# Projected keys and queries of an attention kernel: whole 512-column blocks, four block writes per half, separate staging, queries projected at the end of the attention before

## The chip, the cores and the metric

The kernel runs on one core of a Trainium2 chip. A core has five engines that run their own instruction streams in order: TensorE (PE, matrix products into PSUM), VectorE (DVE), ScalarE (ACT), GpSimd (POOL) and SyncE (SP, which here only starts DMA transfers). ScalarE starts DMA transfers on a queue of its own too. The metric is the device time of one execution in microseconds (us), median of three runs.

## The reference

The input x is 4 images of 256 channels by 64 × 64 = 4096 positions, in float32. Two layers follow each other. The second one is told in words only, since the change doesn't touch what it computes.

```python
xf = x.reshape(B, C, N)                                  # 4, 256, 4096
q = jnp.einsum('oc,bcn->bno', wq, xf) + bq               # 32 channels
k = jnp.einsum('oc,bcn->bon', wk, xf) + bk[None, :, None]  # 32 channels
attn = jax.nn.softmax(jnp.einsum('bnd,bdm->bnm', q, k), axis=-1)
v = jnp.einsum('oc,bcn->bon', wv, xf) + bv[None, :, None]  # 256 channels
out = jnp.einsum('bcn,bmn->bcm', v, attn).reshape(B, C, H, W)
y = gamma[0] * out + x
```

The second layer: a group norm, a context cluster block (features and values of 4 heads × 24 channels, split in four folds of 32 × 32 positions, similarity of each position to four centres, a hard assignment to the best one, aggregation, projection back to 256 channels, added with a factor), a second group norm, an MLP 256 → 1024 → 256 with GELU, added with a factor, and at the end batch norms, ReLU and a 256 × 256 pointwise product.

## The kernel before, in words

**Order.** The order of all engines' work is written out by hand (`tc.manual_schedule`): each engine takes its instructions in the order in which the Python code issues them, and waits on semaphores where data or a buffer is not ready. The images run one after the other. Each has an attention stage, a cluster stage (with group norm 1), and an MLP stage (with group norm 2), and work of the next image is put into the gaps of the last two.

**Attention.** An image has 8 query blocks of 512 positions (`nb`) and 8 key groups of 512 positions (`g`). A unit `u` is one pair of these, 64 in all. For each unit `score` (L386 on) multiplies four 128-key slices with the query block on TensorE (sc, L395), and ScalarE copies the result from PSUM to a slot of the pool `spool` (tag "s"), while VectorE keeps a running maximum. `exps` (L500, L503) subtracts the maximum on VectorE and takes the exponential on ScalarE, POOL adds up the denominators (L505, L508), and `weigh` (L513) multiplies by the values on TensorE into PSUM (av). Scores run 10 units ahead of the weighting (`LEAD`). `weighting` is the loop over all 64 units; it loads x of the next image at its end (`ahead`) and the weights of the following stages (`load_mix`, `load_mlp`).

**Split operands.** Keys and queries have 32 channels. Both are held as a rounded part (hi) and the rest (lo), and stacked on 128 partitions: four row groups c of 32 rows, in which keys are hi, lo, hi, lo and queries hi, hi, lo, lo. One product over 128 rows then gives the sum of all four products of the parts.

**Projection and stacking.** `k_half(i)` projects the keys of half an image (2048 positions): 32 rows in each of four row groups r of a PSUM tile (from the pool `ps_m`, 2 banks), each row group holding other positions. `halves_of` forms hi on ScalarE (L298) and lo on VectorE (L299). Since each row group holds other positions, the stacking goes through DRAM: 16 transfers of 64 KB (row group c of the stack by row group r of the projection, L326) on SP's queue write the DRAM tile [128, 4096], and `k_unit` (L381) and `q_block` (L375) load blocks [128, 512] from it. `q_four(i)` does the same for four query blocks (L356, L367). hi and lo of a key half, and those of queries of the first half, share one SBUF tile with the tag "acc" and one buffer, which is the tag of the denominators too. So the next half's hi waits until the 16 writes before it have landed.

**Where these stand.** For image 0, `alone()` runs `k_half(0)`, `q_four(0)`, the first loads, four v pairs (L337 on TensorE, copied by ScalarE at L345), and then eight score units, each followed by a v pair; `k_half(1)` stands before unit 3. For later images, the list `projections` has 32 v half steps, in which `k_half(0)` and `q_four(0)` stand after the 16th and `k_half(1)` after the 26th counted with these; `fill(n)` takes the next n of the list at fixed places of the stages of the image before (tail of the attention, group norms, cluster, first part of the MLP). In every image, `q_four(1)` stands after unit 17 of its own attention.

Of the kernel before, what the change touches and what calls it, by code (L numbers as in the profile page):

```python
# [8 lines left out]
F32 = mybir.dt.float32  # L9
F32R = mybir.dt.float32r  # L10
# [36 lines left out]
def attention_then_cluster_block(  # L47
# [229 lines left out]
    def attention(b, xs):  # L277
# [4 lines left out]
        cells = small.tile([P, KC, NBLK, 4], F32, tag="cells", name=f"cells_{b}")  # L282
        qs, ks, slots, mxs, accs, tops, rdens, ts = {}, {}, {}, {}, {}, {}, {}, {}

        def halves_of(ps, bias, tags, name):

            if len(tags) == 1:  # L290
                both = work.tile([P, 2, NB], F32R, tag=tags[0], bufs=1, name=f"hl_{name}")
                hi, lo = both[:, 0], both[:, 1]
            else:
                hi, lo = (
                    work.tile([P, NB], F32R, tag=t, bufs=1, name=f"hl{j}_{name}")
                    for j, t in enumerate(tags)
                )
            nc.scalar.activation(hi, ps, AF.Identity, bias=bias)  # L298
            nc.vector.scalar_tensor_tensor(  # L299
                lo, ps, bias, hi.bitcast(F32), ALU.add, ALU.subtract  # L300
            )
            return hi, lo

        def k_half(i):

            if i == 0:
                own["k"] = dram.tile([P, N], F32, tag="k", name=f"k_{b}")
                own["q"] = dram.tile([P, N], F32, tag="q", name=f"q_{b}")
            ps = ps_m.tile([P, NB], F32, tag="m", name=f"kp_{b}_{i}")
            for t in range(2):  # L310
                for k in range(KC):
                    for r in range(RG):
                        nc.tensor.matmul(
                            ps[r * D : (r + 1) * D, t * 2 * P : (t + 1) * 2 * P],
                            wqk_s[:, k, 1],
                            xs[2 * i + t][:, k].rearrange("p (g r n) -> p r g n", g=2, r=RG)[:, r],
                            start=(k == 0),
                            stop=(k == KC - 1),
                        )
            parts = halves_of(ps, bqk_s[:, 1:2], ("acc",), f"k_{b}_{i}")  # L320
            cols = own["k"][:, i * N // 2 : (i + 1) * N // 2]
            for c in range(4):
                rows = cols[c * D : (c + 1) * D].rearrange("d (g r n) -> d r g n", r=RG, n=P)
                src = parts[c % 2].bitcast(F32).rearrange("p (g n) -> p g n", n=P)
                for r in range(RG):
                    nc.sync.dma_start(out=rows[:, r], in_=src[r * D : (r + 1) * D])  # L326

        vps = {}

# [18 lines left out]
            v_half(2 * i)  # L348
            v_half(2 * i + 1)

        def q_four(i, tags=("acc",)):

            ps = ps_m.tile([P, NB], F32, tag="m", name=f"qp_{b}_{i}")
            for k in range(KC):
                for r in range(RG):
                    nc.tensor.matmul(  # L356
                        ps[r * D : (r + 1) * D],
                        wqk_s[:, k, 0],
                        block(xs, k, 4 * i + r),
                        start=(k == 0),  # L360
                        stop=(k == KC - 1),
                    )
            parts = halves_of(ps, bqk_s[:, 0:1], tags, f"q_{b}_{i}")
            for c in range(4):
                for r in range(RG):
                    o = (4 * i + r) * NB
                    nc.sync.dma_start(  # L367
                        out=own["q"][c * D : (c + 1) * D, o : o + NB],
                        in_=parts[c // 2][r * D : (r + 1) * D].bitcast(F32),
                    )  # L370

        def q_block(nb):

            qs[nb] = work.tile([P, NB], F32R, tag="q", name=f"q_{b}_{nb}")
            nc.sync.dma_start(out=qs[nb].bitcast(F32), in_=own["q"][:, nb * NB : (nb + 1) * NB])  # L375

        def k_unit(u):

            g = u % GRP
            ks[u] = big.tile([P, NB], F32R, tag="k", bufs=2, name=f"k_{b}_{u}")  # L380
            nc.sync.dma_start(out=ks[u].bitcast(F32), in_=own["k"][:, g * NB : (g + 1) * NB])  # L381

        def score(u, hooks=None, later=None):

# [181 lines left out]

        def alone():

            k_half(0)
            q_four(0)  # L570
            k_unit(0)
            q_block(0)
            q_block(1)
            for i in range(4):
                v_pair(i)
            for u in range(GRP):
                if u == RG - 1:
                    k_half(1)
                hooks, maxima = [], []
                score(u, hooks, maxima)  # L580
                for f in hooks + maxima:
                    f()
                v_pair(u + 4)
            fold(0)
            for i in range(GRP + 4, GRP + 6):
                v_pair(i)
            half["dg"] = across(0)
            v_pair(GRP + 6)
            spread(0, half["dg"])
            v_pair(GRP + 7)  # L590
            exps(0)
            score(GRP)
# [23 lines left out]
                if p % GRP == GRP - 1:  # L616
                    fold(p // GRP)

        def weighting(ahead, fill, early):
            mb, av = None, None  # L620

            biased = {u: (i // KC, i % KC) for i, u in enumerate((3, 4, 5, 6, 20, 28, 36, 44))}
            for u in range(units):
                nb, g = divmod(u, GRP)
                more = nb + 1 < NBLK
                if g == 0:
                    av = [
                        ps_a.tile([P, NB], F32, tag=f"a{c}", name=f"av{c}_{b}_{nb}")
                        for c in range(KC)
                    ]  # L630
                if g + 1 < GRP:
                    exps(u + 1)
                else:
                    gather(nb)
                p = u + LEAD
                if u == units - 4:
                    load_mix(b)
                    load_mlp(b)
                elif u == units - 1:
                    turn_mlp()  # L640
                due(u, 0)
                if p - units > 1:
                    ahead()
                if g == GRP - 1 and more:
                    exps(u + 1)
                weigh(u, av, 0)
                due(u, 1)
                weigh(u, av, 1)
                if nb:
                    if g == 0:  # L650
                        total(nb - 1)
                    elif g == 3:
                        add(nb - 1)
                    elif g == 5:
                        seen(nb - 1)
                    elif g == 7:
                        pooled(nb - 1)
                due(u, 2)
                weigh(u, av, 2)
                if g == GRP - 2 and more:  # L660
                    known(nb + 1, mb)
                due(u, 3)
                if g == GRP - 3 and more:
                    mb = highest(nb + 1)
                weigh(u, av, 3)
                if u == 1:
                    early()
                if u in biased:

                    t, c = biased[u]  # L670
                    nc.scalar.activation(
                        xs[t][:, c], xs[t][:, c], AF.Identity, bias=gbv[:, c : c + 1]
                    )
                if u == 2 * GRP + 1:
                    q_four(1, ("w2", "q4"))
                if g == 3 and nb + 2 < NBLK:
                    q_block(nb + 2)
                if g == GRP - 1 and more:
                    clear(nb, av)
# [41 lines left out]
        parts.score, parts.fold, parts.q_block, parts.k_unit = score, fold, q_block, k_unit  # L721
        parts.maximum, parts.first, parts.exps = maximum, first, exps
        parts.projections = [lambda i=i: v_half(i) for i in range(N // P)]
        parts.projections[26:26] = [lambda: k_half(1)]
        parts.projections[16:16] = [lambda: k_half(0), lambda: q_four(0)]
        return parts


# [872 lines left out]
    with tc.manual_schedule():  # L1601
# [3 lines left out]
        for b in range(B):  # L1605
            xs1, begun = [], []
            nxt = attention(b + 1, xs1) if b + 1 < B else None

            def ahead():
                if nxt and len(xs1) < N // XT:  # L1610
                    xs1.append(load_x(b + 1, len(xs1)))
                elif late and not begun:
                    begun.append(begin())

            begin, todo, gelu = late or (None, list(nxt.projections) if nxt else [], lambda i: None)
            fill = filler(todo)
            stats, cells, rest = here.weighting(ahead, fill, (lambda: None) if b else derived)
            turned = turn_w2(b, not nxt)
            maxima = []
            stats2 = cluster(b, here.xs, stats, cells, rest, fill, gelu, nxt, maxima)  # L1620

            late = mlp(b, here.xs, stats2, fill, nxt, NBLK - (b == B - 2), turned, maxima)
            here = nxt
# [76 lines left out]
```

## Time and profile before

| | |
|---|---|
| time, median of 3 runs | 3352.77 us (3351.12 to 3354.02) |
| time of the profiled execution | 3354.39 us |
| span of the profiled execution | 3352.4 us |
| mean granted TensorE clock | 0.985 |
| TensorE busy | 3236.9 us, 97% of the span |
| VectorE, POOL, ScalarE busy | 2231.0, 1930.9, 1678.8 us |
| key writes `k<-hl_k` | 128 of 64 KB, 1.8 us from issue to landing |
| query writes `q<-hl_q` | 128 of 64 KB, 1.7 us |
| key loads `k<-k` | 256 of 256 KB, 3.0 us |
| query loads `q<-q` | 32 of 256 KB, 3.2 us |

The profile is one execution, recorded by the hardware profiler. Busy time counts the instructions of an engine; the chain of work that ended last is followed back from the last instruction to what released each step. A wait line names the waiting instruction, the one that released it, and then the sum in us, the number of waits and the longest. A timeline line has the start in us from the span's beginning, the duration of the group, the engine and line, the operation, output and inputs, shape and number of instructions; in square brackets stands the idle time before it and what ended it. SPq stands for SP's DMA queue. Names such as kp, qp (projections in PSUM), hl_k, hl_q (their parts), sc (scores), vp (projected values), av (weighted values) are the kernel's tiles without numbers.

### The profile page before, as it was taken

To read this page: it belongs to the slowest core of one execution; us is meant where nothing else is said; L and a number is where in the kernel's file an instruction comes from. 1 tells how busy PE (TensorE), PEld (TensorE's weight loads), DVE (VectorE), ACT (ScalarE), POOL (GpSimd) and SP (SyncE) were. 2 spreads that over 40 slices of the span, in tenths; PEclk is the share of its full clock that TensorE was granted. 3 is DMA by queue.
4 is the path that set the end of the run, shared out by engine and by line. 5 is a ranking of instruction groups with operands and counts; after the bars stand their busy time and mean duration, and the time that the engine had idled before them with its cause. 6 is when DMAs were issued, how large, how long until landed. Compare 5 with 4: busy or idle time off the path is not lost.

```text
span 3352.4 us, 33609 instructions
## 1 busy us (share of the span) xinstructions
PE 3236.9 (97%) x11242; PEld 1943.3 (58%) x11242; DVE 2231.0 (67%) x3570; ACT 1678.8 (50%) x2253; POOL 1930.9 (58%) x1358
## 2 busy tenths in 40 slices
PE   5999999899999999989999999998999999999999
PEld 4444444688644444468864444456884444446786
DVE  2767775567676677466767677746776767765675
ACT  3655553445565555344556455534455555544444
POOL 0566667266466667636636567663664666673664
PEclk8999999999999999999999999999999999999999
DMA  4121112110111111210011111122011121110000
GB/s 141 38 66 38 48 51 87 32 26 29 44 54 54 47 44 41 87 44 24 29 44 51 52 43 54 41 77 48 20 38 54 43 61 38 47 52 1 13 20 26
DMA packets 103133, 154.83 MB, mean 46 GB/s; under 512 B 16336, under 2 KB 41520, under 8 KB 102960
## 3 DMA queue, kind: packets, MB, share of 16 engines
q1 hardware_dynamic: 101936, 151.56, 14.5%
q8 instruction: 89, 1.46, 0.2%
q10 hardware_dynamic: 1024, 1.12, 0.1%
q14 instruction: 84, 0.69, 0.1%
HBM read 118.96 MB, written 33.67 MB: 46 GB/s over the span
## 4 chain that ended last, share of the span: by engine, by line
PE 89%; DVE 4%; SPq 2%; ACT 1%; DMA 1%; issue 1%; POOL 1%; ACTq 0%; DVEq 0%; POOLq 0%
PE av L513 50%; PE mo L1331 9%; PE sc L395 7%; PE hq L1414 5%; PE hp L1414 3%; PE hr L1414 3%; PE fv L910 3%; PE vp L337 2%; PE mo L1315 1%; SPq L326 1%; SPq L367 1%; PE hq_pw L1414 1%; PE pw L1270 1%; PE hr_pw L1414 1%; PE hp_pw L1414 1%
## 5 line engine op out<-in xcount | busy, mean ns | idle before, releaser
L513 PE MATMUL av<-s,v 128*128 128x512 f32 x4096 | 1800.1, 593 | 0.7 <-ACT s L503 0.7
L508 POOL TENSOR_TENSOR acc<-acc,s 128x1024 f32<-128x1024 f32 x448 | 1060.3, 2367 | 500.7 <-ACT s L503 480.3
L513 PEld LDWEIGHTS av<-s,v 128*128 128x128 f32 x4096 | 778.3, 190 | 898.4 <-issue 868.8
L503 ACT ACTIVATE s<-s 128x1024 f32<-128x1024 f32 x512 | 541.0, 1058 | 600.6 <-DVE s L500 580.4
L500 DVE TENSOR_TENSOR s<-s,mb 128x1024 f32<-128x1024 f32 x512 | 595.7, 1205 | 17.4 <-ACT mb L484 15.8
L421 DVE TENSOR_TENSOR top<-sc,top 128x1024 f32<-128x1024 f32 x196 | 239.1, 1220 | 304.0 <-PE sc L395 304.0
L1369 ACT ACTIVATE hs<-hs,pv_s 128x256 f32<-128x256 f32 x496 | 232.5, 503 | 342.8 <-DVE hs L1405 342.8
L395 PE MATMUL sc<-q,k 128*128 128x512 f32 x1024 | 370.9, 484 | 30.9 <-DMA k<-k 24.6
L1331 PE MATMUL mo<-hs,w 128*128 128x256 f32 x1512 | 385.1, 381 | 0.0
L1331 PEld LDWEIGHTS mo<-hs,w 128*128 128x128 f32 x1512 | 283.9, 190 | 46.1 <-ACT hs L1369 6.6
L424 DVE TENSOR_TENSOR top<-sc,top 128x1024 f32<-128x1024 f32 x196 | 240.1, 1225 | 82.2 <-ACT s L417 69.5
L395 PEld LDWEIGHTS sc<-q,k 128*128 128x128 f32 x1024 | 191.1, 191 | 174.4 <-issue 127.4
L417 ACT COPY s<-sc 128x1024 f32<-128x1024 f32 x224 | 224.7, 1003 | 128.5 <-PE sc L395 109.2
L422 ACT COPY s<-sc 128x1024 f32<-128x1024 f32 x224 | 227.6, 1016 | 110.5 <-DVE top L421 74.4
L1405 DVE TENSOR_TENSOR hs<-hq,hs 128x256 f32<-128x256 f32 x496 | 198.3, 421 | 79.2 <-PE hq L1414 68.8
L505 POOL TENSOR_TENSOR acc<-s 128x1024 f32<-128x1024 f32 x32 | 75.9, 2372 | 291.8 <-ACT s L503 291.8
L1338 POOL TENSOR_TENSOR hs<-hs 128x256 f32<-128x256 f32 x108 | 82.4, 763 | 183.0 <-ACT hs L1422 86.0
L337 PE MATMUL vp<-wv_s,x 128*128 128x256 f32 x512 | 137.7, 417 | 39.9 <-ACT v L345 39.3
L337 PEld LDWEIGHTS vp<-wv_s,x 128*128 128x128 f32 x512 | 102.3, 207 | 67.5 <-ACT v L345 43.2
L1414 PE MATMUL hr<-xn,w 128*128 128x256 f32 x496 | 128.4, 381 | 0.5 <-DVE hs L1405 0.5
L1405 DVE TENSOR_TENSOR hs<-hp,hs 128x256 f32<-128x256 f32 x124 | 52.1, 420 | 115.1 <-ACT hs L1422 115.1
L1047 POOL TENSOR_TENSOR x<-cl,x 128x512 f32<-128x512 f32 x32 | 40.0, 1278 | 120.6 <-ACT cl L1046 120.6
(263 smaller groups left out, 3566.3 us busy)
## 6 DMA issues: line engine op xcount, KB each, us to landing
k<-k SPq DMA_DIRECT2D x256, 256.0 KB, 3.0
out<-xn SPq DMA_DIRECT2D x62, 256.0 KB, 2.2
x<-in_x SPq DMA_DIRECT2D x30, 512.0 KB, 6.2
k<-hl_k SPq DMA_DIRECT2D x128, 64.0 KB, 1.8
q<-hl_q SPq DMA_DIRECT2D x128, 64.0 KB, 1.7
q<-q SPq DMA_DIRECT2D x32, 256.0 KB, 3.2
w<-in_w SPq DMA_DIRECT2D x8, 1024.0 KB, 10.1
mr<-row_mx SPq DMA_DIRECT2D x28, 256.0 KB, 3.5
```

Source lines behind the costliest of these rows:

```text
L337: nc.tensor.matmul(vps[0][:, i % 2, :], xs[i * P // XT][:, k, o : o + P], wv_s[:, k, :], start=(k == 0), stop=(k == KC - 1),)
L395: nc.tensor.matmul(halves[r // 2][:, r % 2, :], k_s[:, r * P : (r + 1) * P], q_s, start=True, stop=True,)
L421: nc.vector.tensor_tensor(top, halves[1], top, ALU.max)
L424: nc.vector.tensor_tensor(top, halves[0], top, ALU.max)
L500: nc.vector.tensor_tensor(sh, sh, mxs[nb].unsqueeze(1).to_broadcast([P, 2, NB]), ALU.subtract)
L503: nc.scalar.activation(sh, sh, AF.Exp)
L508: nc.gpsimd.tensor_tensor(acc, acc, s[:, 2 * h : 2 * h + 2], ALU.add)
L513: nc.tensor.matmul(av[c], own["v"][:, RG * g + quarter, c * P : (c + 1) * P], slots[u][:, quarter, :], start=(g == 0 and quarter == 0), st ...
L1331: return nc.tensor.matmul(bank[:, half * HB : (half + 1) * HB], a[:, j], t, start=start, stop=stop)
L1369: nc.scalar.activation(src, src, AF.Gelu_apprx_tanh, bias=pvc("b1", P, j + 4 * (i > 1)))
L1405: nc.vector.tensor_tensor(dst, ps, term, ALU.add)
L1414: nc.tensor.matmul(out, w, x, start=True, stop=True)
```

## The change

The projection, the split and the writes of a half are now one function, `halves_of`, used for keys and queries alike. The keys too are projected by matmuls of 512 columns, one position block in each row group. The DRAM tile is [8, 4, 32, 512], so that each block [128, 512] is contiguous, and a half is written by four transfers of 256 KB, one per row group c of the stack, each over all 128 partitions of hi or of lo. `staged` projects two halves into the two banks of one score PSUM tile (pool `ps_s`) and keeps their hi and lo apart in the four quarters of one slot of `spool`. `keys(i)` keeps hi and lo of a key half in the two "k" buffers.

In image 0, `staged("first")` has the first halves of keys and queries, written on ScalarE's queue, `staged("second")` has the second halves, at unit 0, written on SP's queue, and six v pairs instead of four stand ahead of the units. For later images, the key halves stay in the list of fill steps at the same indices, while all eight query blocks are projected by `staged("queries")` after unit 61 of the attention of the image before (`prepare`). The list has one step less, and `q_four(1)` after unit 17 is gone.

```diff
@@ -282,48 +282,49 @@
         cells = small.tile([P, KC, NBLK, 4], F32, tag="cells", name=f"cells_{b}")
         qs, ks, slots, mxs, accs, tops, rdens, ts = {}, {}, {}, {}, {}, {}, {}, {}
-        def halves_of(ps, bias, tags, name):
-            if len(tags) == 1:
-                both = work.tile([P, 2, NB], F32R, tag=tags[0], bufs=1, name=f"hl_{name}")
-                hi, lo = both[:, 0], both[:, 1]
-            else:
-                hi, lo = (
-                    work.tile([P, NB], F32R, tag=t, bufs=1, name=f"hl{j}_{name}")
-                    for j, t in enumerate(tags)
-                )
+        def halves_of(which, i, parts, ps, dma=nc.sync):
+            col = 1 if which == "k" else 0
+            if which not in own:
+                own[which] = dram.tile([NBLK, 4, D, NB], F32, tag=which, name=f"{which}_{b}")
+            for k in range(KC):
+                for r in range(RG):
+                    nc.tensor.matmul(
+                        ps[r * D : (r + 1) * D],
+                        wqk_s[:, k, col],
+                        block(xs, k, 4 * i + r),
+                        start=(k == 0),
+                        stop=(k == KC - 1),
+                    )
+            bias = bqk_s[:, col : col + 1]
+            hi, lo = parts
             nc.scalar.activation(hi, ps, AF.Identity, bias=bias)
             nc.vector.scalar_tensor_tensor(
                 lo, ps, bias, hi.bitcast(F32), ALU.add, ALU.subtract
             )
-            return hi, lo
-        def k_half(i):
-            if i == 0:
-                own["k"] = dram.tile([P, N], F32, tag="k", name=f"k_{b}")
-                own["q"] = dram.tile([P, N], F32, tag="q", name=f"q_{b}")
+            rows = own[which][4 * i : 4 * i + 4]
+            for c in range(4):
+                part = hi if c in ((0, 2) if which == "k" else (0, 1)) else lo
+                dma.dma_start(out=rows[:, c], in_=part.bitcast(F32))
+        def staged(name, which, dma=nc.sync):
+            st = spool.tile([P, 4, NB], F32R, tag="s", name=f"st_{b}_{name}")
+            ps = ps_s.tile([P, 2, NB], F32, tag="s", name=f"pr_{b}_{name}")
+            for j, (w, i) in enumerate(which):
+                halves_of(w, i, (st[:, 2 * j], st[:, 2 * j + 1]), ps[:, j], dma)
+        def keys(i):
             ps = ps_m.tile([P, NB], F32, tag="m", name=f"kp_{b}_{i}")
-            for t in range(2):
-                for k in range(KC):
-                    for r in range(RG):
-                        nc.tensor.matmul(
-                            ps[r * D : (r + 1) * D, t * 2 * P : (t + 1) * 2 * P],
-                            wqk_s[:, k, 1],
-                            xs[2 * i + t][:, k].rearrange("p (g r n) -> p r g n", g=2, r=RG)[:, r],
-                            start=(k == 0),
-                            stop=(k == KC - 1),
-                        )
-            parts = halves_of(ps, bqk_s[:, 1:2], ("acc",), f"k_{b}_{i}")
-            cols = own["k"][:, i * N // 2 : (i + 1) * N // 2]
-            for c in range(4):
-                rows = cols[c * D : (c + 1) * D].rearrange("d (g r n) -> d r g n", r=RG, n=P)
-                src = parts[c % 2].bitcast(F32).rearrange("p (g n) -> p g n", n=P)
-                for r in range(RG):
-                    nc.sync.dma_start(out=rows[:, r], in_=src[r * D : (r + 1) * D])
+            parts = [
+                big.tile([P, NB], F32R, tag="k", bufs=2, name=f"hl{j}_{b}_{i}") for j in range(2)
+            ]
+            halves_of("k", i, parts, ps)
         vps = {}
@@ -348,37 +349,16 @@
             v_half(2 * i)
             v_half(2 * i + 1)
-        def q_four(i, tags=("acc",)):
-            ps = ps_m.tile([P, NB], F32, tag="m", name=f"qp_{b}_{i}")
-            for k in range(KC):
-                for r in range(RG):
-                    nc.tensor.matmul(
-                        ps[r * D : (r + 1) * D],
-                        wqk_s[:, k, 0],
-                        block(xs, k, 4 * i + r),
-                        start=(k == 0),
-                        stop=(k == KC - 1),
-                    )
-            parts = halves_of(ps, bqk_s[:, 0:1], tags, f"q_{b}_{i}")
-            for c in range(4):
-                for r in range(RG):
-                    o = (4 * i + r) * NB
-                    nc.sync.dma_start(
-                        out=own["q"][c * D : (c + 1) * D, o : o + NB],
-                        in_=parts[c // 2][r * D : (r + 1) * D].bitcast(F32),
-                    )
         def q_block(nb):
             qs[nb] = work.tile([P, NB], F32R, tag="q", name=f"q_{b}_{nb}")
-            nc.sync.dma_start(out=qs[nb].bitcast(F32), in_=own["q"][:, nb * NB : (nb + 1) * NB])
+            nc.sync.dma_start(out=qs[nb].bitcast(F32), in_=own["q"][nb].rearrange("c d n -> (c d) n"))
         def k_unit(u):
             g = u % GRP
             ks[u] = big.tile([P, NB], F32R, tag="k", bufs=2, name=f"k_{b}_{u}")
-            nc.sync.dma_start(out=ks[u].bitcast(F32), in_=own["k"][:, g * NB : (g + 1) * NB])
+            nc.sync.dma_start(out=ks[u].bitcast(F32), in_=own["k"][g].rearrange("c d n -> (c d) n"))
         def score(u, hooks=None, later=None):
@@ -566,24 +546,21 @@
         def alone():
-            k_half(0)
-            q_four(0)
+            staged("first", (("k", 0), ("q", 0)), nc.scalar)
             k_unit(0)
             q_block(0)
             q_block(1)
-            for i in range(4):
+            for i in range(6):
                 v_pair(i)
             for u in range(GRP):
-                if u == RG - 1:
-                    k_half(1)
+                if u == 0:
+                    staged("second", (("k", 1), ("q", 1)))
                 hooks, maxima = [], []
                 score(u, hooks, maxima)
                 for f in hooks + maxima:
                     f()
-                v_pair(u + 4)
+                v_pair(u + 6)
             fold(0)
-            for i in range(GRP + 4, GRP + 6):
-                v_pair(i)
             half["dg"] = across(0)
             v_pair(GRP + 6)
             spread(0, half["dg"])
@@ -616,7 +593,7 @@
                 if p % GRP == GRP - 1:
                     fold(p // GRP)
-        def weighting(ahead, fill, early):
+        def weighting(ahead, fill, early, prepare):
             mb, av = None, None
             biased = {u: (i // KC, i % KC) for i, u in enumerate((3, 4, 5, 6, 20, 28, 36, 44))}
@@ -671,8 +648,8 @@
                     nc.scalar.activation(
                         xs[t][:, c], xs[t][:, c], AF.Identity, bias=gbv[:, c : c + 1]
                     )
-                if u == 2 * GRP + 1:
-                    q_four(1, ("w2", "q4"))
+                if u == units - 3:
+                    prepare()
                 if g == 3 and nb + 2 < NBLK:
                     q_block(nb + 2)
                 if g == GRP - 1 and more:
@@ -721,8 +698,9 @@
         parts.score, parts.fold, parts.q_block, parts.k_unit = score, fold, q_block, k_unit
         parts.maximum, parts.first, parts.exps = maximum, first, exps
         parts.projections = [lambda i=i: v_half(i) for i in range(N // P)]
-        parts.projections[26:26] = [lambda: k_half(1)]
-        parts.projections[16:16] = [lambda: k_half(0), lambda: q_four(0)]
+        parts.projections[26:26] = [lambda: keys(1)]
+        parts.projections[16:16] = [lambda: keys(0)]
+        parts.prepare = lambda: staged("queries", (("q", 0), ("q", 1)))
         return parts
@@ -1614,7 +1592,9 @@
             begin, todo, gelu = late or (None, list(nxt.projections) if nxt else [], lambda i: None)
             fill = filler(todo)
-            stats, cells, rest = here.weighting(ahead, fill, (lambda: None) if b else derived)
+            stats, cells, rest = here.weighting(
+                ahead, fill, (lambda: None) if b else derived, nxt.prepare if nxt else lambda: None
+            )
             turned = turn_w2(b, not nxt)
             maxima = []
             stats2 = cluster(b, here.xs, stats, cells, rest, fill, gelu, nxt, maxima)
```

## The prediction

> **What bounds the kernel now.** I read the page's chain first, then TensorE's waits, then the timeline of each place where the change touches TensorE's order. The chain:
>
> ```profile
> PE 89%; DVE 4%; SPq 2%; ACT 1%; DMA 1%; issue 1%; POOL 1%; ACTq 0%; DVEq 0%; POOLq 0%
> ```
>
> TensorE is busy 3236.9 of 3352.4 us, so an edit pays only as far as it shortens TensorE's own work or its roughly 115 us of gaps. The waits (total us, times, longest) name the gaps of these helpers:
>
> ```profile
> PE vp L337 <- ACT v L345: 39.3, 8, 12.7
> PE sc L395 <- DMA k<-k: 24.6, 5, 10.4
> ...
> PE sc L395 <- DMA q<-q: 4.3, 1, 4.3
> ```
>
> By window, the 39.3 is 12.9 at the start and 9.0, 8.1 and 9.2 in the three passages from one image to the next. ScalarE, named as releaser, is itself held: over all engines `ACT hl_q L298 <- DMA k<-hl_k` is 44.3 us in 4 waits. The timeline of the first passage shows it:
>
> ```profile
> 631.01 1.93 PE L313 MATMUL kp<-x,wqk_s 128*32 128x256 f32 x32
> 632.77 1.90 PE L356 MATMUL qp<-x,wqk_s 128*32 128x512 f32 x16
> 635.25 8.66 SPq L326 DMA_DIRECT2D k<-hl_k  x16
> 645.45 0.69 ACT L298 ACTIVATE hl_q<-qp,bqk_s 128x512 fp32r<-128x512 f32 x1 [10.22 <-DMA k<-hl_k]
> 646.66 3.78 PE L337 MATMUL vp<-wv_s,x 128*128 128x256 f32 x8 [8.61 <-ACT v L345]
> 652.37 3.02 PE L940 MATMUL agg<-vf,sim 128*32 128x96 f32 x64 [1.93 <-DVE sim L870]
> ```
>
> The query half needs the "acc" tile that the key half's 16 writes still read. ScalarE stands 10.2 us; the v copy behind it frees no PSUM bank; TensorE stops. In the middle of an attention (columns as above):
>
> ```profile
> 234.86 1.92 PE L356 MATMUL qp<-x,wqk_s 128*32 128x512 f32 x16
> 237.65 7.37 SPq L367 DMA_DIRECT2D q<-hl_q  x16
> 248.26 1.17 PE L395 MATMUL sc<-q,k 128*128 128x512 f32 x4 [3.49 <-DMA k<-k]
> ```
>
> Here 16 issues hold SP's queue 7.4 us and the next key load is late. And the start:
>
> ```profile
> 19.44 7.72 SPq L326 DMA_DIRECT2D k<-hl_k  x16
> 28.69 0.69 ACT L298 ACTIVATE hl_q<-qp,bqk_s 128x512 fp32r<-128x512 f32 x1 [14.32 <-DMA k<-hl_k]
> 29.41 7.37 SPq L367 DMA_DIRECT2D q<-hl_q  x16
> 42.14 2.04 PE L395 MATMUL sc<-q,k 128*128 128x512 f32 x4 [4.34 <-DMA q<-q]
> 54.40 7.92 SPq L326 DMA_DIRECT2D k<-hl_k  x16
> 66.85 2.05 PE L395 MATMUL sc<-q,k 128*128 128x512 f32 x4 [10.37 <-DMA k<-k]
> 90.80 3.70 PE L513 MATMUL av<-s,v 128*128 128x512 f32 x8 [0.70 <-ACT s L503]
> ```
>
> Up to the first av at 90.8 everything is a serial chain of writes, loads and eight score units.
>
> [...] granted clock 0.50 from 645 to 655 us, and x8 vp matmuls take 3.78 instead of 1.99 us, agg 3.02 instead of 1.50.
>
> **The price of the new write** is the main unknown. 256 KB over four engines is 32 packets of 2 KB each. Near rows: from 813.5 to 816.5, among 2 KB rows, 215 GB/s at DMA share 0.67, so 20 GB/s per engine, 100 ns per packet; the old query writes, two packets per engine at a time, showed 14.6 GB/s (140 ns)[...]; 4 KB rows at 549 to 560 gave 25 GB/s. I take 20: 3.3 us per write, 13 us per half, 26 for two halves. Ends: 2.6 us (25 GB/s) and 4.5 us (14.6 GB/s).
>
> **Part 1: the query half at u = 17 goes** (four attentions). Its matmuls are 1.9 us; the stall behind is 3.49 here and 3.8, 3.4 and 3.5 in the others. 5.4 × 4 = −21.5.
>
> **Part 2: the passage** (three). `keys(0)` has its own two "k" buffers and no query half follows, so the v copy isn't held. The chain from kp to agg(sim), 631.0 to 652.4 = 21.4 us, falls to TensorE's issue of kp, vp, agg(pool_w) and then VectorE's sim chain (5.5 us), which I put at 10.6 in all, with 2.9 us of TensorE idle left: −10.8. [...] the slow clock mostly goes: −1. The fill list is one item shorter, which takes half a v pair out of the MLP's batch: −0.9. About −12.7.
>
> Hidden in it: the 13 us of key writes from about 635 end at 650; `k_0` lands near 657.5 and score(0) needs it at about 662 to 666. Cover some 8 us, gone at about 5 us per write. `keys(1)` waits for the same buffers at about 657: covered by 7 us. The first load behind its writes is for score(1), some 60 us of MLP later.
>
> **Part 3: `prepare()` at u = 61** (three). Two projections at 1.75 us, in TensorE's continuous av run (busy to 590.2), plus a stall where the second half waits for VectorE's lo of the first (both share one PSUM tile: 0.69 + 0.75 and latencies): 1.7. +5.2. ScalarE and VectorE carry two more operations each ahead of the last exponentials, which then end near 586.8 for TensorE's need at 588.5; POOL's last sum ends near 591.6 for the den matmul at 595.3: hidden by 1.7 and 3.7 us. SP issues eight writes; nothing else is in its queue from 563 to 635, and they land by about 606, before the slot's next owner (near 625). Parts 2 and 3: −7.5 × 3 = −22.
>
> **Part 4: the start.** Keys' hi is ready at 14.4; their writes leave on ACT's queue, not behind mix_first, which gains 5 us; but eight writes on four engines take 26.2 us, and ACT's later issues wait for landings of SP's early loads, for which I add 4 to 5: queries land at about 46, `q_0` 3.2 later, score(0) at 49.3 (before: 42.1). `staged("second")` stands ahead of it on TensorE and SP, so its eight writes run from 47 to 75, and `k_1` is behind them: score(1) at 76 (before: 46.1). No key gap follows at unit 4. From score(1): six units at 2.65 us, the pace of 46.09 to 48.75, and 13.4 from score(7) to the first av, as 77.37 to 90.80: 76 + 29.3 is about 105.5, +15. With 2.6 us per write +4, with 4.5 +35 at most: 16 writes in series, 16.5 us per us of the price.
>
> **Sum:** −21.5 − 22 + 15 = −28.5. The profiled execution took 3354.4 with a span of 3352.4; the median is 3352.8. So 3352.8 − 28.5 = 3324.
>
> **Rivals.**
> *All 16 engines carry the writes.* Then a half takes about 4 us, score(1) is at 46.5 as before, the gap at unit 4 goes and first av is at about 74: −17. Total −60: 3292. For it: nothing in this trace shows a transfer on four engines. [...]
> *Loads aren't held by earlier writes.* `k_1` passes them; start −3, total −46: 3306.
> *The passage gives less*: slow writes at 4.5 us, or the gap refilled by VectorE's chain and `prepare()` at double price (+5 × 3): 3335 to 3346.
> *Slower than before: the price of a write at four engines is 5 us or more.* From there the start alone costs 43.5 and eats all the rest (13.1 GB/s per engine, just under the old writes' 14.6). At 6 us: +45 on my sum, 3369. The packets would have to run slower in long rows than in short ones.
>
> **How the numbers follow.** Main case (2.6 to 4 us per write) 0.46, 3313 to 3336; sixteen engines 0.13; loads pass 0.09; passage less 0.20; slow writes 0.12. The likeliest is 3324. The range 3290 to 3350 leaves out the slow writes and the tail of sixteen engines. 0.2% is 6.7 us, about what a measurement of this kernel can tell from no change; below 3346 lie all but the slow writes and a strip of 0.05: faster 0.83, same 0.05, slower 0.12.
>
> **What would show it.** Right: one write on four engines in 3 to 4 us, DMA share near 0.25 from 15 to 75 us, score(1) at 70 to 85 and first av at 100 to 112; no query projection near u = 17 and no key wait of 3.5 there; kp to agg(sim) near 10.6 us; a wait of about 1.7 us at the second query projection. Wrong: DMA share near 1 at the start and first av near 74 (sixteen engines); first av beyond 120; a new wait of den or av at an attention's end; `k_0` late at score(0) of the next image.

## The result and the profile after

| | before | after |
|---|---|---|
| median of 4 runs | 3352.61 us (3351.12 to 3354.02) | 3314.82 us (3314.09 to 3316.30) |
| ratio | | 0.9888, 95% interval 0.9871 to 0.9905 |
| span of the profiled execution | 3352.4 us | 3314.5 us |
| first av product | 90.80 us | 99.85 us |
| mean granted TensorE clock | 0.985 | 0.991 |

The changed kernel is 37.8 us faster. The forecast was 3324, so it had the direction and most of the size; its sum was 9 us short.

The names of the products that serve as marks below: kp is the first product of a key half, den the one that ends an attention, agg(sim) the first product of the cluster stage that needs VectorE's similarities, gnm_gn the first of the second group norm, and hp the first of the MLP. A passage is the stretch from den to hp, with the next image's projections in it.

The chain is TensorE's as before, without the two SPq terms of 1% each. From the page's chain of the changed kernel:

```profile
PE 90%; DVE 5%; DMA 1%; ACT 1%; issue 1%; POOL 1%; SPq 0%; ACTq 0%; DVEq 0%; POOLq 0%
```

TensorE's waits in the changed kernel (us in total, times, longest):

```profile
PE sc L375 <- DMA k<-k: 19.4, 3, 18.3
PE vp L338 <- ACT v L346: 14.2, 4, 12.2
...
PE pr_queries L295 <- DVE st_queries L305: 5.0, 3, 1.7
```

The 39.3 us of vp behind ScalarE's copies are 14.2, nearly all at the start. Of the key waits one, 18.3 us, holds nearly everything, also at the start. The last line is new: the second query projection after unit 61.

**The passage.** Timeline of the changed kernel, first passage (start, us, engine, line, operation):

```profile
639.53 1.92 PE L295 MATMUL kp<-x,wqk_s 128*32 128x512 f32 x16
649.98 1.97 PE L918 MATMUL agg<-vf,sim 128*32 128x96 f32 x64 [2.35 <-DVE sim L848]
```

From kp to agg(sim) are 10.45 us, where 21.36 were. The idle time left is VectorE's, 2.35 us, and agg runs in 1.97 instead of 3.02.

**The attention's end.** Timeline of the changed kernel:

```profile
579.42 1.92 PE L295 MATMUL pr_queries<-x,wqk_s 128*32 128x512 f32 x16
582.18 13.18 SPq L311 DMA_DIRECT2D q<-st_queries  x8
583.00 1.92 PE L295 MATMUL pr_queries<-x,wqk_s 128*32 128x512 f32 x16 [1.65 <-DVE st_queries L305]
598.78 0.43 PE L663 MATMUL den<-rden,ones 128*32 128x128 f32 x8
```

The wait of 1.65 us is there; no wait of av or den follows.

**The start.** Timeline of the changed kernel:

```profile
14.31 3.83 ACTq L311 DMA_DIRECT2D k<-st_first  x4
27.50 4.72 ACTq L311 DMA_DIRECT2D q<-st_first  x4
44.70 3.24 SPq L311 DMA_DIRECT2D k<-st_second  x4
47.37 0.73 PE L375 MATMUL sc<-q,k 128*128 128x512 f32 x2
48.22 10.06 SPq L311 DMA_DIRECT2D q<-st_second  x4
58.33 46.76 SPq L361 DMA_DIRECT2D k<-k  x11
69.78 2.04 PE L375 MATMUL sc<-q,k 128*128 128x512 f32 x4 [18.28 <-DMA k<-k]
99.85 3.70 PE L493 MATMUL av<-s,v 128*128 128x512 f32 x8 [0.71 <-ACT s L483]
```

Score(1) begins at 69.78 instead of 46.09. SP's four query writes alone take 10.06 us to issue, and key 1 is behind them. The windows of the changed kernel (window, its length, busy time and count of PE, PEld, DVE, ACT and POOL, then granted clock, DMA share, GB/s) show how wide the query writes of the first half run:

```profile
35.00:40.00 5.00, 5.00 (x20) 4.19 (x20) 0.00 (x0) 1.17 (x2) 0.53 (x1) 0.80 0.26 102
```

102 GB/s at a share of 0.26 of 16 engines, about what four of them show if they are busy throughout (16 times 0.26 is 4.2). By this estimate each moves 25 GB/s, and 64 KB per engine take 2.6 us.

**Where the 37.9 us of span went**, between anchors of TensorE (first av, each den product, each first MLP product hp), in the order of the stages:

| term | change, us | forecast |
|---|---|---|
| start to first av | +9.05 | +15 |
| attentions, without the projections after unit 61 | −5.7, −8.3, −7.2, −7.6 = −28.8 | −21.5 |
| three times after unit 61: 2 × 1.75 + 1.65 | +15.5 | +15.6 |
| three passages, den to hp: 90.96, 88.24, 90.72 to 78.04, 79.95, 79.97 | −32.0 | −35.4 |
| MLPs with the next scores, hp to av | −0.6 | −2.7 |
| after the last den | −1.0 | 0 |

The attention terms are av-to-den spans (499.47, 501.43, 499.79 and 499.76 before; 498.93, 498.25, 497.77 and 492.16 after), from which the 5.15 us after unit 61 are taken where they occur. The 5.15 is the sum of two products and one wait, read from the timeline.

### The profile page after: what moved, and what is told of

It is laid out like the page before. It is cut to its first block, busy times and chain, and to the rows that moved or that the text cites. A ratio compares the mean times of both kernels' runs of the same rounds, so it can differ in the third digit from the quotient of the medians.

```text
span 3314.5 us, 33083 instructions
## 1 busy us (share of the span) xinstructions
PE 3220.7 (97%) x11114; PEld 1930.3 (58%) x11114; DVE 2231.4 (67%) x3570; ACT 1679.6 (51%) x2253; POOL 1929.9 (58%) x1358
## 4 chain that ended last, share of the span: by engine, by line
PE 90%; DVE 5%; DMA 1%; ACT 1%; issue 1%; POOL 1%; SPq 0%; ACTq 0%; DVEq 0%; POOLq 0%
PE av L493 52%; PE mo L1309 9%; PE sc L375 7%; PE hq L1392 5%; PE hp L1392 3%; PE hr L1392 3%; PE fv L888 3%; PE vp L338 2%; PE mo L1293 1%; PE hq_pw L1392 1%; DVE st L993 1%; PE pw L1248 1%; PE hr_pw L1392 1%; PE hp_pw L1392 1%; DMA k<-k 1%
## 5 line engine op out<-in xcount | busy, mean ns | idle before, releaser
L338 PE MATMUL vp<-wv_s,x 128*128 128x256 f32 x512 | 133.1, 407 | 14.2 <-ACT v L346 14.2
L1392 PEld LDWEIGHTS hr<-xn,w 128*128 128x128 f32 x496 | 94.4, 191 | 18.0 <-issue 3.3
```

The costliest lines, as they stand in the source:

```text
L338: nc.tensor.matmul(vps[0][:, i % 2, :], xs[i * P // XT][:, k, o : o + P], wv_s[:, k, :], start=(k == 0), stop=(k == KC - 1),)
L1392: nc.tensor.matmul(out, w, x, start=True, stop=True)
```

## The experiments

**One: width of the writes.** A layout in which the writes have 128 rows outermost, where the changed kernel's have four blocks, and the loads 32 rows; the number of transfers, their bytes and their places stay.

```diff
-own[which] = dram.tile([NBLK, 4, D, NB], ...)
+own[which] = dram.tile([2, 4, P, NB], ...)
-rows = own[which][4 * i : 4 * i + 4]
+rows = own[which][i]
-dma.dma_start(out=rows[:, c], in_=part.bitcast(F32))
+dma.dma_start(out=rows[c], in_=part.bitcast(F32))
+def stacked(which, nb):
+    r = nb % RG
+    return own[which][nb // RG][:, r * D : (r + 1) * D].rearrange("c d n -> d c n")
-in_=own["q"][nb].rearrange("c d n -> (c d) n")
+in_=stacked("q", nb)
-in_=own["k"][g].rearrange("c d n -> (c d) n")
+in_=stacked("k", g)
```

Keys and queries are then stacked row by row (d, c) instead of (c, d), which changes nothing in their product.

> The changed kernel with one other DRAM layout: [2, 4, 128, 512], so that each of the four writes of a half goes from 128 partitions to 128 rows of one stride [...], and the loads read 32 rows of four row groups each (32 outermost). Count of transfers, their bytes and all places stay. Theory (four engines carry the new writes, and the start pays for it): the writes take about 1 us of their engines instead of 2.6, key 1 is not held, the 18.3 us wait at the start goes, first av near 72 to 76 instead of 99.9, total 3287 to 3293. Rival (the start's loss comes from the place and the order of the writes, not from their width): first av stays near 95 to 100, total within 5 us of 3315.

Measured: 3290.10 us, ratio to before 0.9813 (0.9798 to 0.9827). Timeline of this kernel's start:

```profile
36.38 1.78 SPq L311 DMA_DIRECT2D q<-st_second  x4
...
38.21 36.82 SPq L366 DMA_DIRECT2D k<-k  x11
41.81 1.17 PE L380 MATMUL sc<-q,k 128*128 128x512 f32 x4 [2.16 <-DMA k<-k]
...
69.60 3.70 PE L498 MATMUL av<-s,v 128*128 128x512 f32 x8 [0.71 <-ACT s L488]
```

The windows show the width best after unit 61, where no other transfer is in SP's queue. First the changed kernel, then this one:

```profile
586.00:596.00 10.00, 10.00 (x24) 4.38 (x24) 3.85 (x4) 3.60 (x4) 7.03 (x4) 1.00 0.26 102
554.00:556.00 2.00, 2.00 (x17) 0.56 (x10) 0.00 (x0) 0.24 (x1) 0.00 (x0) 1.00 1.02 379
```

The share of 0.26 has become 1.02, and 102 GB/s have become 379. In the traces' semaphore records the changed kernel's eight writes land there 2.56 us apart and this kernel's 0.7. At the start four issues take 1.78 us instead of 10.06, the 18.3 us wait is 2.16, and the first av comes 30 us earlier than in the changed kernel. The three passages' kp to agg(sim) stay at 10.45. So the start pays for the width, and the width is worth 25 us of the whole. (Of the start's 30 us some 4 come back in this trace, spread over the four attentions, and under 2 in a second trace of the same kernel; why was not tried.)

**Two: number of transfers.** The changed kernel with 16 transfers of 64 KB per half.

```diff
-dma.dma_start(out=rows[:, c], in_=part.bitcast(F32))
+for r in range(RG):
+    dma.dma_start(out=rows[r, c], in_=part[r * D : (r + 1) * D].bitcast(F32))
```

> The changed kernel with 16 transfers of 64 KB per half (32 partitions to 32 rows, as before the change), in the same places and queues. Theory (the count of transfers is worth nothing in itself away from the start, since their issue is hidden): passages and attention as in the changed kernel, kp to agg(sim) near 10.5 us. At the start 32 issues on ScalarE's queue at 0.55 us and 32 on SP's at 0.45 us take the place of the slow writes: first av 92 to 100, total 3307 to 3316. Rival (fewer transfers are what the change lives on): 3325 or more.

Measured: 3310.66 us, ratio 0.9875 (0.9860 to 0.9889). The first av is at 94.35, kp to agg(sim) at 10.45, 10.45 and 10.44. After unit 61, SP issues for 14.89 us and no one waits for it. The timeline of its start shows what the issues cost there:

```profile
13.90 11.38 ACTq L312 DMA_DIRECT2D k<-st_first  x16
...
46.12 7.44 SPq L312 DMA_DIRECT2D k<-st_second  x16
...
53.66 7.43 SPq L312 DMA_DIRECT2D q<-st_second  x16
61.13 38.45 SPq L362 DMA_DIRECT2D k<-k  x11
64.11 2.04 PE L376 MATMUL sc<-q,k 128*128 128x512 f32 x4 [11.19 <-DMA k<-k]
```

With sixteen narrow writes to a half score(1) begins at 64.11 us, with the changed kernel's four at 69.78. Where the changed kernel has them, fewer transfers showed no gain outside the start (kp to agg(sim) 10.45 us with both); at the start 16 issues hold the queue about as long as four slow writes do (7.43 us for each half, against 3.24 and 10.06). At the old place after unit 17 the 16 issues did cost; that is experiment four.

**Three: the passage's wait alone**, in the kernel before. The query half's hi and lo get the two key buffers, for the passages only.

```diff
-parts.projections[16:16] = [lambda: k_half(0), lambda: q_four(0)]
+parts.projections[16:16] = [lambda: k_half(0), lambda: q_four(0, ("k", "k"))]
 ...
+    big.tile([P, NB], F32R, tag=t, bufs=2, name=f"hl{j}_{name}")
+    if t == "k" else
     work.tile([P, NB], F32R, tag=t, bufs=1, name=f"hl{j}_{name}")
```

> The kernel before with one edit: in the passages the query half keeps hi and lo in the two key buffers instead of the tile that the key half's writes still read. The 16 writes per half, the query half at unit 17 and the start stay. Theory (the passage's gap is ScalarE's wait for the key writes to land): kp to agg(sim) falls from 21.4 to about 12, three times about 9 us and 1 to 2 of slow clock, total 3320 to 3328. Rival (the gain of the passage comes from fewer transfers or from the query half's leaving): at most 8 us faster, 3344 or more.

Measured: 3323.91 us, ratio 0.9913 (0.9898 to 0.9928). Timeline of its first passage:

```profile
630.32 1.93 PE L315 MATMUL kp<-x,wqk_s 128*32 128x256 f32 x32
...
634.43 0.67 ACT L300 ACTIVATE hl_q<-qp,bqk_s 128x512 fp32r<-128x512 f32 x1
634.55 8.61 SPq L328 DMA_DIRECT2D k<-hl_k  x16
...
641.42 3.02 PE L942 MATMUL agg<-vf,sim 128*32 128x96 f32 x64 [2.33 <-DVE sim L872]
```

ScalarE takes the query half at once, beside the same 16 writes, and kp to agg(sim) is 11.1 us in all three. The three passages, den to hp, are 29.5 us shorter than before (240.4 instead of 269.9), where the changed kernel has 32.0. The wait for the shared tile was the passage's gap.

**Four: unit 17's stall alone**, in the kernel before: the projection stays and the 16 writes are issued four at a time.

```diff
-q_four(1, ("w2", "q4"))
+held = []
+q_four(1, ("w2", "q4"), held)      # issues the first 4, leaves 3 groups of 4 in held
+elif 2 * GRP + 1 < u < 2 * GRP + 5:
+    held.pop(0)()
-if g == 3 and nb + 2 < NBLK:
+if g == (4 if nb == 2 else 3) and nb + 2 < NBLK:
```

> The kernel before with one edit: of the 16 writes of the query half at unit 17, four are issued after each of units 17, 18, 19 and 20, so that SP is held under 2 us at a time and the key load is not late; the query load of block 4 goes one unit later. The projection itself stays (1.75 us each). Theory from the trace (the stall of 3.5 us also puts TensorE's clock to half for some us in three of four attentions): the stall's 14.2 us go and some 7 more, total 3329 to 3334. Rival (the stall costs only its length): 3337 to 3340.

Measured: 3330.53 us, ratio 0.9933 (0.9916 to 0.9950). No key wait is left in the attentions. The av-to-den spans fall by 3.1, 6.3, 4.9 and 5.3, in sum 19.6 us; the stalls taken away were 3.49, 3.84, 3.41 and 3.49, in sum 14.2. The other 5.4 are in what followed a stall: nothing in image 0, and 2.5, 1.5 and 1.8 us in images 1 to 3. (Another 2.7 us of this run's gain is in a start that the edit doesn't touch and that moves by as much between runs.) The windows of the kernel before around the stall of image 1:

```profile
1065.00:1070.00 5.00, 4.51 (x11) 1.71 (x9) 4.11 (x5) 3.42 (x5) 4.42 (x2) 1.00 0.55 133
1070.00:1073.00 3.00, 0.00 (x0) 0.00 (x0) 0.91 (x1) 1.92 (x2) 2.31 (x2) 0.92 0.72 212
1073.00:1076.00 3.00, 2.65 (x5) 1.82 (x6) 0.57 (x1) 1.01 (x1) 2.92 (x3) 0.50 0.27 102
1076.00:1079.00 3.00, 3.00 (x5) 1.35 (x4) 2.90 (x3) 1.01 (x1) 2.92 (x2) 0.50 0.28 87
```

and its timeline at the same place:

```profile
1073.35 2.05 PE L395 MATMUL sc<-q,k 128*128 128x512 f32 x4 [3.84 <-DMA k<-k]
1075.19 9.11 PE L513 MATMUL av<-s,v 128*128 128x512 f32 x16
1083.74 1.49 PE L395 MATMUL sc<-q,k 128*128 128x512 f32 x4
1085.06 7.03 PE L513 MATMUL av<-s,v 128*128 128x512 f32 x16
```

After 3.84 us of idleness the clock stands at 0.50, and the same 16 av products take 9.11 instead of 7.03 us. In the clock records half clock lasts there from 1072.5 to 1079.4 us, and 3.4 us behind the stalls of images 2 and 3; half of the time in which TensorE worked at it is 3.0, 1.7 and 1.7 us, about what the experiment won beyond the stalls. Image 0's stall of 3.49 at 248 us, which the prediction showed, was followed by a full clock and 7.03: images 1 to 3 paid, image 0 did not.

**Five: key 1's place in the queue.** The changed kernel with the load of key 1 ahead of the second halves' writes.

```diff
 if u == 0:
+    k_unit(1)
     staged("second", (("k", 1), ("q", 1)))
 ...
-if u + 1 < units:
+if u + 1 < units and u + 1 not in ks:
     k_unit(u + 1)
```

> The changed kernel with the load of key block 1 issued ahead of the eight writes of the second halves in image 0, nothing else. Theory (the load of key 1 came late because it stood behind these writes [...]): score(1) near 50 to 52 instead of 69.8; the load for unit 2, issued at score(1), is now the one behind the writes and comes at about 69 to 71, so the first av is only 2 to 4 us earlier than 99.9. Rival (the load waits for something else than its place, such as the data of the first half): score(1) stays within 3 us of 69.8.

Measured once: 3316.0 us, first av at 99.31. Timeline of its start:

```profile
44.63 0.43 SPq L361 DMA_DIRECT2D k<-k  x1
...
51.21 1.28 PE L375 MATMUL sc<-q,k 128*128 128x512 f32 x4
59.35 20.04 SPq L361 DMA_DIRECT2D k<-k  x5
70.82 2.05 PE L375 MATMUL sc<-q,k 128*128 128x512 f32 x4 [16.60 <-DMA k<-k]
```

Score(1) is 18.6 us earlier, and the wait has moved whole to the next unit, whose key is now the one behind the writes. The place was the cause of key 1's delay. The first av gains 0.5 us, less than the 2 to 4 expected. One unit of 2.65 us less is left behind the wait, but the wait ends 1 us later, and from 91.6 to 95.0 us the granted clock is 0.50, where it is 1.00 in the changed kernel.

**Six: the shared PSUM tile.** Experiment one with the two query projections in two tiles; it was run twice, the second time beside experiment one on the same chip.

```diff
 for j, (w, i) in enumerate(which):
+    if j and name == "queries":
+        ps = ps_s.tile([P, 2, NB], F32, tag="s", name=f"pr1_{b}_{name}")
     halves_of(w, i, (st[:, 2 * j], st[:, 2 * j + 1]), ps[:, j], dma)
```

> The kernel of e1_wide with the two query projections after unit 61 in two PSUM tiles instead of two banks of one. Theory (the second projection's wait of 1.65 us is for VectorE's reading of the first bank, because both share one tile): that wait goes in all three passages, 5 us, total 3283 to 3287. Rival (something else holds it, or the last exponentials are then late for TensorE): within 2 us of 3290, with a wait of av or den in the trace.

Measured: 3285.85 us, ratio 0.9814 (0.9797 to 0.9830). The ratio is that of experiment one on its own chip, so this settles nothing on the time. Hence again, with experiment one as the base:

> e1_wide once more, beside the two kernels derived from it and on the same chip, since e1_wide was compared on another chip than they: the base, ratio to the kernel before near 0.981.

> e5_wide_two once more beside e8_wide. Theory (TensorE's three waits of 1.65 us are gone and nothing takes their place): 3 to 6 us under e8_wide. Rival (the time comes back elsewhere, such as in slow clock after gaps that fall differently): within 2 us of e8_wide.

Measured: base 3290.10 (3288.38 to 3293.29), ratio 0.9824 (0.9810 to 0.9838); two tiles 3284.65 (3280.57 to 3287.89), ratio 0.9804 (0.9790 to 0.9818). The medians are 5.5 us apart and the times don't overlap, while the intervals of the ratios do. The timeline of the second run shows that the wait is gone:

```profile
551.37 3.64 PE L295 MATMUL pr_queries<-x,wqk_s 128*32 128x512 f32 x32
```

Both projections run as one, and no wait of av or den follows. So the shared tile caused the wait. That its three times 1.65 us are the 5.5 us of the medians fits, and is as sure as the medians are.

**Seven: the place at the attention's end.** Experiment one with the queries where they stood before the change, in buffers of their own and with four wide writes each.

```diff
+def queries(i):
+    ps = ps_m.tile([P, NB], F32, tag="m", ...)
+    parts = [work.tile([P, NB], F32R, tag=t, bufs=1, ...) for t in ("w2", "q4")]
+    halves_of("q", i, parts, ps)
-if u == units - 3:
-    prepare()
+if b and u == 2 * GRP + 1:
+    queries(1)
-parts.projections[16:16] = [lambda: keys(0)]
+parts.projections[16:16] = [lambda: keys(0), lambda: queries(0)]
```

> The kernel of e1_wide with the queries of images 1 to 3 where they stood before the change: the first half behind the key half in the passage, with its own buffers, the second after unit 17 of its own attention; four 16-engine writes each; nothing after unit 61. Theory (moving the queries to the attention's end gains nothing of itself; it was the held SP queue that cost at unit 17, and the shared tile in the passage): the 5.2 us after unit 61 go three times, 1.75 us come back at unit 17 without a stall and 0.7 to 2 in the passage, total 3280 to 3287. Rival (the place at the attention's end is what gains): key waits or slow clock come back near unit 17 or in the passage, 3292 or more.

Measured: 3280.62 us (3276.25 to 3288.33), ratio 0.9799 (0.9783 to 0.9814). Beside the base on one chip:

> e6_mid once more beside e8_wide. Theory (with writes that don't hold SP's queue, the place at the attention's end gains nothing): 4 to 10 us under e8_wide. Rival (the place gains): at or over e8_wide.

Measured: 3284.62 us (3282.36 to 3288.46), ratio 0.9806 (0.9792 to 0.9820), median 5.5 us under the base; the intervals of the ratios overlap here too. There is no stall near unit 17. Kp to agg(sim) is 11.11 instead of 10.45, and agg(sim) to hp is 30.35, 28.56 and 30.17 instead of 28.02 each, which gives some of the gain back. Moving the queries to the end gains nothing of itself: by the medians it is some 5 us dearer here than their old place, about as much as the shared tile costs. This kernel and the one with two tiles are the fastest, 2% under the kernel before, and can't be told apart.

## Why the prediction was right, and by how much each step missed

*Part 2, the passage.* The mechanism was right and so was its main term: 10.9, 10.0 and 11.1 us of kp to agg(sim), where −10.8 was forecast, with 2.35 us of TensorE idleness left where I put 2.9. Experiment three shows the shared tile's wait as the cause. The three passages with the MLP behind them gave −32.6 instead of −38. What was over-sized is the small change: "−1" of slow clock and "−0.9" of the shorter list, three times each. From agg(sim) to hp the changed kernel needs 26.84, 28.75 and 28.78, where 28.86, 27.02 and 28.43 were needed: image 0 won 2 us and image 1 lost nearly as much. What failed is the assumption behind the "−1", that the shorter gap leaves the clock alone. In image 0 half clock follows the 2.35 us gap ahead of agg(sim) (651.4 to 654.8 us). In images 1 and 2 it follows a gap of only 1.85 us ahead of gnm_gn, and in image 0 the same gap has no such effect:

```profile
673.11 0.38 PE L248 MATMUL gnm_gn<-mv_gn,left 128*128 128x1 f32 x2 [1.85 <-DVE mv_gn L246]
1484.01 0.41 PE L248 MATMUL gnm_gn<-mv_gn,left 128*128 128x1 f32 x2 [1.85 <-DVE mv_gn L246]
```

```profile
673.50:680.00 6.50, 5.57 (x26) 4.38 (x27) 4.25 (x14) 3.02 (x6) 2.05 (x2) 1.00 0.24 72
1485.00:1491.00 6.00, 6.00 (x16) 4.83 (x16) 3.71 (x13) 2.52 (x5) 1.45 (x2) 0.50 0.24 75
```

So the same gap was followed by half clock in two images and by full clock in one. (At full clock agg(sim) takes 1.76 us in images 1 and 2; the 1.50 that the prediction set against 3.02 was too low.)

*Part 1, unit 17.* This is the term that was mis-sized most: −28.8 instead of −21.5. The step priced the stall at its length. Traces and experiment four show that such a stall cost 1.5 to 2.7 us beyond its length in images 1 to 3, and next to nothing in image 0. I had counted slow clock for the passage's gap (0.50 from 645 to 655 us) and not for these stalls. The sign of the extra cost was in the trace of before, and I didn't look at the av groups behind each stall.

*Part 4, the start.* The mechanism was right in each link: a quarter of the engines (share 0.26), key 1 held behind the second halves' writes (18.3 us in the changed kernel; in experiment five, with key 1 ahead of them, score(1) came 18.6 us earlier), no gap at unit 4 after that. That the new writes would go over four engines was an assumption of mine, which the trace before didn't show. The share of 0.26 agrees with it, and in experiment one, where only the DRAM layout and the transfers' patterns with it differ, the share is 1.02.

Mis-sized was the price: the second halves' writes land 2.56 us apart, where I put 3.3. For 2.6 I gave +4 (+3.4 by my own 16.5 us per us of price), and +9.05 came. Three things make up the rest. The first halves' writes had all landed at 42.96 us, where 14.4 and eight times 2.6 and the 4 to 5 that I added make 39.7: the key writes landed 2.8 to 3.6 us apart beside SP's loads, and ScalarE issued the first query write only at 27.50. From the second halves' first issue to score(1) (44.70 to 69.78) are 25.1 us, of which eight writes take 20.6; I had left 2.6 for what stands around them. And the clock was at half until 74.5 us, so that score(1) took 2.04 us. These are about 3.3, 1.9 and 0.8 us.

*Part 3, after unit 61.* As forecast: +5.15, of which 1.65 is the shared tile, and both covers held. The last exponentials end at 589.8 us and no av product waits for them; POOL's last sum ends at 593.6, some 5 us ahead of den. (Den stands at 598.8 where I wrote 595.3, since the start's loss and unit 17's gain move the whole attention 3.4 us later; that accounts for 589.8 instead of 586.8 too.)

*The sum* came out 9.4 us short of the gain, from two misses of one sign (start 6, unit 17 7.3) and one of the other (passages with their MLPs 5.5). That they partly cancel is luck. The rival with the price of 5 us or more was out by a factor of two; the rival of sixteen engines (3292) is what experiment one builds, and it gave 3290.

## What to carry to other kernels

Look at the DMA share of a transfer that a change makes new: joining 16 writes into four with four blocks outermost gave writes at a share of 0.26, and a layout with 128 rows outermost, at 1.02, was worth another 25 us. A buffer shared by two steps that have nothing to do with each other stops the engine that has to wait for it, and what is in order behind it (here ScalarE for 10.2 us and TensorE for 8.6 in a passage); giving the second step its own buffer, in one edit, made most of the gain (28.9 us in experiment three). A stall of TensorE can cost more than its length (three of four near 3.5 us did, by 1.5 to 2.5 us in experiment four), so price it with the products that follow it.

## What the runs showed that I had not expected

A DMA's issue itself can be long: after unit 61 the query writes at a share of 0.26 took 0.5 to 5.0 us each to issue (median 1.19), the same writes in experiment one, at 1.02, 0.32 to 0.45. On ScalarE's queue a write that couldn't be issued yet held the engine's own work: at the start its first v copy waited 13.4 us for the four query writes, and TensorE 12.2 us for it; in experiment one the copy waited 3.5. Here the issues themselves were short (0.52 to 0.60 us). The first three stood until the last increment of the semaphore that they name had come from an earlier transfer: increments at 27.42, 29.12 and 30.98 us, issues at 27.50, 29.14 and 31.06.

One kernel's executions can differ by 12 us (experiment seven: 3276.25 to 3288.33), and its profiled execution was the slowest of them. The slower of its four executions, the lower its mean granted clock, from 0.997 to 0.993. The stage that moves most between profiled executions is that from agg(sim) to hp, 26.06 to 30.35 us over all kernels here.

What decides where the clock falls was not shown. In the kernel before, the stalls at unit 17 of images 1 to 3 (3.84, 3.41 and 3.49 us) went with half clock for 6.8, 3.4 and 3.4 us, and that of image 0, 3.49 us too, with none. In the changed kernel the gap of 1.85 us ahead of gnm_gn (1.86 in image 2) was followed by half clock for 6.8 us in each of images 1 and 2, and by full clock in image 0. No run moved a gap on purpose.
